# Two transformer layers over 16 sequences: the rotary of the second sequence on GpSimd, the squares of the first group's slots on ScalarE, the second group routed later

## The chip, the cores and the metric

The kernel runs on one core of one Trainium2 chip. The metric is the device time of one execution in microseconds (us). Three runs of the kernel before took 1694.8, 1696.43 and 1696.84 us; the median is 1696.43.

## The reference

`x` has 16 sequences of 512 tokens of width 128, in float32. Two layers follow each other. Each makes `x = x + attention(norm(x)) + ffn(norm(x))`.

```python
# layer 0
q, k, v = heads of xn @ Wq.T, xn @ Wk.T, xn @ Wv.T      # 16 heads of width 8
rot(x) = concat(x1 * c - x2 * s, x1 * s + x2 * c)       # rotary, halves of 4; of q and k
q, k = elu(rot(q)) + 1, elu(rot(k)) + 1
y_t = q_t . sum_{s<=t}(k_s v_s) / max(q_t . sum_{s<=t} k_s, 1e-6)     # linear attention, causal
combine = the two largest of softmax(xn @ router_w.T), made to sum to 1, over 8 experts
ffn = sum_e combine[e] * (relu(xn @ w_fc[e].T)**2 @ w_proj[e].T) + the shared expert, likewise
# layer 1
attention: softmax over chunks of 64 queries, a gate from its sums; ffn: a channel mix with the token before
```

Only layer 0 is touched by the change: its rotary, its routing to experts, and the order of its work.

## The kernel before, in words

**Tiling.** A sequence is four tiles of 128 tokens. The 16 sequences are handled in five groups of 3, 4, 4, 3 and 2 (`GROUPS`, line 47). Layer 0 of a group runs beside layer 1 of the group before it. Four chains of work make up the program (lines 1567 to 1595):

- `dispatch(g)` (line 1038) normalizes each sequence of a group (`layernorm_T`: tile `xn`, transposed to `xnT`), makes its router logits (`rt_ps`, `lg`), then routes the group as a whole. `route` (line 671) and `places` (line 718) compute, in some 60 small VectorE operations of at most 128x128, the slot of each token in the buffer of its two experts (`pl_slot`) and the expert of each slot tile (`pl_expert`). Then `send` (line 1087) writes each tile of `xn` to its slots in DRAM (`rows`) by an indirect DMA from GpSimd: 24 of them for group 0, 32 for group 1.
- `slot_tiles(g)` (line 1122) fetches four tiles of slots at a time (`xg`), transposes them (`xgT`), loads the weights of each tile's expert (`wf`, `wp`, 256 KB each, four buffers of each), multiplies (`hg_ps`), takes ReLU and squares (`hg`, in `hidden`, line 1164), multiplies again (`yg_ps`) and writes `results`. Group 0 has 31 such tiles.
- `layer0(g)` (line 1541) runs, sequence by sequence, `linear_operands` (line 827), `linear_attention` (line 917) and `shared_expert` (line 1006). The first two sequences run interleaved (`together`, line 1490), the second with buffers that layer 1 doesn't need yet (`LENT`, line 808).
- `layer1(g)` (line 1553) gathers the expert results back, and runs layer 1.

**The rotary** (lines 846 to 875). TensorE makes q, k and v of two tiles in PSUM (`qkv`). VectorE multiplies q and k by the cosine and by the sine table (`by_cos`, `by_sin`, 128x512 each), joins halves of these into `qr` by a subtraction and an addition (128x256 each), takes the minimum with zero (`phi`). ScalarE takes the exponential; VectorE adds it to the maximum with zero. This is done twice for each sequence. TensorE then makes running sums (`state`) and transposes (`qkT_ps`); scores (`sc`), masked by VectorE (`am`, 128x1024, eight for a sequence); outputs (`o`); transposes (`ho_a`), a division by VectorE (`den`, `o0n`), a transpose (`oh_a`) and the product `y`, with the shared expert's `h`.

**What sets the order.** Every operation is recorded, then emitted by a planner (`Program.run`, line 330) with costs in ns of its own (lines 213 to 222). An operation's rank is the order in which the chains recorded it; the chains are interleaved by due times (lines 1575 to 1583), which are counted in the planner's estimates of each group's length. At each step the planner emits the ready operation of lowest rank on the engine that is free first. On the chip every engine then runs its list strictly in order. So a changed operation or due time can move everything near it. An indirect DMA also waits for TensorE's instruction that was emitted last before it, and two of them are at least 1900 ns of the planner's time apart (line 222). All loads and stores are issued in order by one queue, that of SyncE (SP).

**Buffers.** `xn` has four: the normalization of a fifth sequence waits for the sends of the first. `x_in` has two. In the profile nearly every operation has the line 259, that of the recorder, so groups are told apart by their tiles.

Of the kernel before, what the change touches and what calls it, by code (L numbers as in the profile page):

```python
# [29 lines left out]
F32 = mybir.dt.float32  # L30
I32 = mybir.dt.int32
U32 = mybir.dt.uint32
AF = mybir.ActivationFunctionType
ALU = mybir.AluOpType
AX = mybir.AxisListType

P = 128
B, T, D = 16, 512, 128
# [448 lines left out]
def two_layers(ctx: ExitStack, tc: tile.TileContext, x, small, const, w_fc, w_proj, out):  # L487
    nc = tc.nc
    program = Program(tc)
    V, S, G, M, SP = (  # L490
        program.engine(name, api) for name, api in (
            ("DVE", nc.vector), ("ACT", nc.scalar), ("POOL", nc.gpsimd), ("PE", nc.tensor),
            ("SP", nc.sync),
        )
    )

    def pool(name, bufs, ahead=0, **kw):
        return Pool(
            ctx.enter_context(tc.tile_pool(name=name, bufs=bufs, **kw)), bufs, ahead,
            kw.get("space") == bass.MemoryType.PSUM,  # L500
        )

    fixed = pool("fixed", 1)
    p2 = pool("p2", 2)
# [5 lines left out]
    def big(name):  # L510
        return ps_big.tile([P, 2, 512], F32, tag="big", name=name)
# [16 lines left out]
    def load_x(b, tag, bufs):  # L528
# [4 lines left out]
    passed = {  # L533
        (n, b): memory.tile([P, T], F32, tag=f"{n}{b}", name=f"{n}_{b}")
        for n in ("xnT", "x1") for b in range(B) if n == "x1" or b > 1
    }
# [84 lines left out]
    def by_head(vp):  # L621
        return vp[:, :, 0 : H * (PAIR + 2)].rearrange("p t (h e) -> p t h e", e=PAIR + 2)
# [170 lines left out]
    def tokens_to_heads(o, name, tag):  # L793
# [14 lines left out]
    LENT = {  # L808
        "vpad": 2, "qr": ("ka", 2), "T": ("qa", "qa", 2), "q0m": ("probs", 4), "am": ("ka", 2),
        "oTs": "oTs1", "o": "o1n", "oT": "oT_a1", "xs": ("rr", 2),  # L810
    }
# [15 lines left out]
    def linear_operands(xnT, b, home):  # L827

        vp, vs, states = vpads[home["vpad"]], home["vstrips"], home["states"]
        vh = by_head(vp)
        tag, bufs = home["qr"]
        qr = p2.tile([P, NT, 2 * D], F32, tag=tag, name=f"qr_{b}", bufs=bufs)
        for tp in range(NT // 2):
            pq = big(f"qkv_{b}_{tp}")
            for i in range(2):  # L840
                t = 2 * tp + i
                M.matmul(
                    pq[:, i, 0 : 3 * D], xnT[:, t * P : (t + 1) * P],
                    wqkv0.rearrange("p s d -> p (s d)"), start=True, stop=True,
                )
            ts_ = slice(2 * tp, 2 * tp + 2)
            by_cos = p2.tile([P, 2, 2 * D], F32, tag="by_cos", name=f"by_cos_{b}_{tp}", bufs=1)
            by_sin = p2.tile([P, 2, 2 * D], F32, tag="by_sin", name=f"by_sin_{b}_{tp}", bufs=1)
            qk = pq[:, :, 0 : 2 * D].rearrange("p t (n d) -> p t n d", d=4)
            for o, table in ((by_cos, cos), (by_sin, sin)):  # L850
                V.tensor_tensor(
                    o.rearrange("p t (n d) -> p t n d", d=4), qk,
                    table[:, ts_, :].unsqueeze(2).to_broadcast([P, 2, 2 * H * 2, 4]), ALU.mult,
                )
            v = pq[:, :, 2 * D : 3 * D]
            S.copy(vs[:, ts_, :, 0:PAIR], v.rearrange("p t (s e) -> p t s e", e=PAIR))
            for o in range(2):
                S.copy(
                    vh[:, ts_, o::2, o * DH : (o + 1) * DH],
                    v.rearrange("p t (s o d) -> p t s o d", o=2, d=DH)[:, :, :, o, :],  # L860
                )

            def halves(a):
                return a.rearrange("p t (h two d) -> p (t h) two d", two=2, d=4)

            c, s, r = halves(by_cos), halves(by_sin), halves(qr[:, ts_, :])
            V.tensor_tensor(r[:, :, 0, :], c[:, :, 0, :], s[:, :, 1, :], ALU.subtract)
            V.tensor_tensor(r[:, :, 1, :], s[:, :, 0, :], c[:, :, 1, :], ALU.add)

            x = qr[:, ts_, :]  # L870
            ex = p2.tile([P, 2, 2 * D], F32, tag="by_cos", name=f"phi_{b}_{tp}", bufs=1)
            V.tensor_scalar_min(ex, x, 0.0)
            S.activation(ex, ex, AF.Exp)
            V.scalar_tensor_tensor(x, x, 0.0, ex, ALU.max, ALU.add)
            yield
        yield


        pst = one(f"state_{b}")
        for t in range(NT - 1):  # L880
            M.matmul(
                pst[:, 0 : 8 * (PAIR + 2)], qr[:, t, D : 2 * D],
                vs[:, t, :, :].rearrange("p s e -> p (s e)"),
                start=(t == 0), stop=(t == NT - 2), skip_group_check=True,
            )
            V.tensor_tensor(
                states[t][:, :, 0 : PAIR + 2],
                pst[:, 0 : 8 * (PAIR + 2)].rearrange("p (s e) -> p s e", e=PAIR + 2), blocks,
                ALU.mult,
            )  # L890
        yield

        pts = big(f"qkT_ps_{b}")
        for s in range(2):
            for t in range(NT):
                M.transpose(
                    pts[:, s, t * P : (t + 1) * P], qr[:, t, s * D : (s + 1) * D], ident
                )
        q_tag, k_tag, bufs = home["T"]
        qT = p2.tile([P, T], F32, tag=q_tag, name=f"q0T_{b}", bufs=bufs)  # L900
        S.copy(qT, pts[:, 0, :])
        kT = p2.tile([P, T], F32, tag=k_tag, name=f"k0T_{b}", bufs=bufs)
        S.copy(kT, pts[:, 1, :])
        qms = []
        for u in range(2):
            tag, bufs = home["q0m"]
            qm = (p3 if tag == "probs" else p2).tile(
                [P, 2, T], F32, tag=tag, name=f"q0m_{b}_{u}", bufs=bufs
            )
            for o in range(2):  # L910
                r = 2 * u + o
                S.activation(qm[:, o, :], pts[:, 0, :], AF.Copy, scale=c_("pick")[:, r : r + 1])
            qms.append(qm)
        yield
        return qT, kT, qms
# [206 lines left out]
    def slot_tiles(g):  # L1122
# [3 lines left out]
        _, n_slots = tiles_of(g)  # L1126
# [37 lines left out]
        def hidden(xgT, ws, q, pair):  # L1164
            ph = big(f"hg_ps_{g}_{q}_{pair}")
            for ii, (wf, _) in enumerate(ws):
                i = 2 * pair + ii
                for f in range(NF):
                    M.matmul(
                        ph[:, ii, f * P : (f + 1) * P], wf[:, f * P : (f + 1) * P],  # L1170
                        xgT[:, i * P : (i + 1) * P], start=True, stop=True,
                    )
            h = p2.tile([P, 2, FF], F32, tag="hid", name=f"hg_{g}_{q}_{pair}", bufs=4)
            o = h[:, 0 : len(ws), :]
            S.activation(o, ph[:, 0 : len(ws), :], AF.Relu)

            (V if pair or g == 0 else G).tensor_tensor(o, o, o, ALU.mult)
            return h

        def project(h, ws, n):  # L1180
# [17 lines left out]
        for q in range(-(-n_slots // QUAD)):  # L1198
# [3 lines left out]
            for pair in range(-(-n_quad // 2)):  # L1202
                n = q * QUAD + 2 * pair
# [306 lines left out]
    def head(b):  # L1510

        if not 0 <= b < B:
            return None
        x1 = p2.tile([P, NT, D], F32, tag="x1", name=f"x1_{b}")
        SP.dma_start(x1.rearrange("p t d -> p (t d)"), passed["x1", b])
        yield from combine(x1, b)
        xp = p2.tile([P, T + 1], F32, tag="xp", name=f"xp_{b}", bufs=2)
        G.memset(xp[:, 0:1], 0.0)
        yield from layernorm_T(x1, xp[:, 1 : T + 1], f"1_{b}", "xn1", 1)
        yield  # L1520
        base = yield from channel_mix(x1, xp, b)
        yield
        vp = values(xp[:, 1 : T + 1], b)
        yield
        qm, ka = yield from operands(xp[:, 1 : T + 1], b, 0)
        return xp, base, vp, qm, ka
# [45 lines left out]
    length = [a + b for a, b in zip(*work)]  # L1572
    begin = [sum(length[:g]) for g in range(groups + 1)]
    chains = [[], [], [], []]
    for g, n in enumerate(GROUPS):
        early, late = (begin[g - 1], length[g - 1]) if g else (-length[0], length[0])
        steps = n * (1 + NT) + 3
        chains[0].append((early + 0.1 * late, 0.4 * late / steps, dispatch(g)))
        start = begin[g] - 0.2 * late if g else 0.25 * length[0]
        steps = 5 * -(-tiles_of(g)[1] // QUAD) + 1  # L1580
        chains[1].append((start, (begin[g] + 0.8 * length[g] - start) / steps, slot_tiles(g)))
        chains[2].append((begin[g], length[g] / (n * LAYER_STEPS[0]), layer0(g)))
        chains[3].append((begin[g + 1], length[g + 1] / (n * LAYER_STEPS[1]), layer1(g)))
    jobs = [[c[0][0], c] for c in chains]
    while jobs:
        job = min(jobs, key=lambda j: j[0])
        _, step, steps = job[1][0]
# [102 lines left out]
```

## Time and profile before

The profiled execution took 1693.02 us, of which the span of the trace is 1691.2 (the rest lies ahead of the first and behind the last instruction). The busy time of each engine, in us, in stretches of the span:

| stretch, us | TensorE | VectorE | ScalarE | GpSimd | TensorE clock | DMA, GB/s |
|---|---|---|---|---|---|---|
| 0 to 50 | 22.23 | 36.29 | 15.49 | 12.73 | 0.77 | 174 |
| 50 to 100 | 40.64 | 30.87 | 15.38 | 18.78 | 0.85 | 116 |
| 100 to 150 | 40.19 | 29.21 | 17.12 | 21.51 | 0.86 | 182 |
| 150 to 200 | 49.28 | 25.18 | 17.13 | 15.24 | 1.00 | 239 |
| 200 to 250 | 45.56 | 26.71 | 21.76 | 18.44 | 1.00 | 214 |
| 250 to 300 | 47.04 | 45.28 | 21.07 | 20.40 | 0.93 | 199 |
| 300 to 1550 | 1207.18 | 939.34 | 603.27 | 299.31 | 0.99 | 88 |
| 1550 to 1691.2 | 118.50 | 88.81 | 53.49 | 5.75 | 0.86 | 10 |

How to read what follows. A timeline line gives the start, the duration, the engine, the operation with its tiles (output, arrow, inputs), the shape and the count, and in brackets the idle time of the engine just before and what ended it. The clock is the share of its full rate at which TensorE was let run: at 0.5 a product takes twice as long. DMA share is the mean busy share of 16 DMA engines. The indirect DMAs appear as work of GpSimd (POOL), about 1 us each. Layer 1 starts near 250 us.

### The profile page before, as it was taken

To read this page: it belongs to the slowest core of one execution; us is meant where nothing else is said; L and a number is where in the kernel's file an instruction comes from. 1 tells how busy PE (TensorE), PEld (TensorE's weight loads), DVE (VectorE), ACT (ScalarE), POOL (GpSimd) and SP (SyncE) were. 2 spreads that over 40 slices of the span, in tenths; PEclk is the share of its full clock that TensorE was granted. 3 is DMA by queue.
4 is the path that set the end of the run, shared out by engine and by line. 5 is a ranking of instruction groups with operands and counts; after the bars stand their busy time and mean duration, and the time that the engine had idled before them with its cause. 6 is when DMAs were issued, how large, how long until landed. Compare 5 with 4: busy or idle time off the path is not lost.

```text
span 1691.2 us, 36456 instructions
## 1 busy us (share of the span) xinstructions
PE 1570.6 (93%) x14503; PEld 1035.6 (61%) x14503; DVE 1221.7 (72%) x2520; ACT 764.7 (45%) x1175; POOL 412.2 (24%) x389
## 2 busy tenths in 40 slices
PE   4869999999999999999999999999999999999996
PEld 2658876576766566666666656666665566555443
DVE  7845458878478975986668894968587867677673
ACT  2324434544443644444444654453544543534424
POOL 2426053054114321151013321140115010104000
PEclk8879999999999999999999999999999999999888
DMA  5357775343342442332223242313133223010000
GB/s 166 119 165 227 219 223 177 94 128 106 110 117 88 116 144 70 111 109 77 88 78 95 80 129 76 103 55 117 51 90 92 63 72 100 8 45 28 19 1 13
DMA packets 155129, 167.78 MB, mean 99 GB/s; under 512 B 13264, under 2 KB 100688, under 8 KB 154960
## 3 DMA queue, kind: packets, MB, share of 16 engines
q1 hardware_dynamic: 146768, 148.67, 29.6%
q0 software_dynamic: 8192, 16.79, 3.1%
q8 instruction: 114, 1.87, 0.4%
q14 instruction: 55, 0.45, 0.1%
HBM read 123.59 MB, written 41.81 MB: 98 GB/s over the span
## 4 chain that ended last, share of the span: by engine, by line
PE 55%; DVE 12%; ACT 3%; issue 1%; ACTq 0%; DVEq 0%
PE sc L259 11%; PE o L259 10%; PE st L259 8%; PE yg_ps L259 5%; DVE maxima L259 4%; PE hg_ps L259 4%; PE y L259 4%; PE qk L259 3%; PE h_ps L259 2%; ACT ex L259 1%; PE ho_a L259 1%; PE qkv L259 1%; PE oh_a L259 1%; PE cm_r L259 1%; PE mx L259 1%
## 5 line engine op out<-in xcount | busy, mean ns | idle before, releaser
L259 DVE TENSOR_REDUCE maxima<-sc 128x2 f32<-128x768 f32 (+2 forms) x448 | 385.4, 913 | 73.9 <-PE sc L259 70.9
L259 ACT ACTIVATE ex<-st 128x1024 f32<-128x1024 f32 x320 | 312.4, 1025 | 184.8 <-PE st L259 175.5
L259 PE MATMUL sc<-ka,qa 32*128 32x512 f32 (+2 forms) x1792 | 213.8, 516 | 7.2 <-DVE maxima L259 3.5
L259 PE MATMUL st<-qa,ka 32*128 32x384 f32 (+3 forms) x2048 | 208.8, 466 | 9.2 <-ACT ex L259 4.6
L259 DVE TENSOR_TENSOR am<-sc,const_sb 128x1024 f32<-128x1024 f32 x128 | 151.3, 1218 | 86.4 <-PE sc L259 82.7
L259 PEld LDWEIGHTS yg_ps<-wp,hg 128*128 128x128 f32 x1304 | 161.9, 194 | 52.6 <-issue 33.4
L259 PE MATMUL yg_ps<-wp,hg 128*128 128x128 f32 x1304 | 184.1, 285 | 8.2 <-DVE hg L259 1.9
L1091 POOL DMA_INDIRECT rows<-xn,pl_slot x128 | 135.9, 1061 | 205.2 <-PE y L259 38.4
L259 PE MATMUL hg_ps<-xgT,wf 128*128 128x128 f32 x1304 | 176.9, 282 | 7.3 <-DVE maxima L259 2.4
L1110 POOL DMA_INDIRECT back<-results,pl_slot x128 | 129.6, 1013 | 213.9 <-PE st L259 45.5
L259 PEld LDWEIGHTS hg_ps<-xgT,wf 128*128 128x128 f32 x1304 | 160.1, 195 | 30.9 <-issue 13.6
L259 PE MATMUL o<-ex,vpad 128*32 128x512 f32 (+3 forms) x2048 | 174.6, 443 | 1.0 <-ACT oT_a L259 0.6
L259 PEld LDWEIGHTS st<-qa,ka 32*128 32x128 f32 x2048 | 103.3, 185 | 78.7 <-issue 27.9
L259 ACT ACTIVATE hg<-hg_ps 128x1024 f32<-128x1024 f32 x84 | 84.0, 1000 | 123.4 <-PE hg_ps L259 108.7
L259 POOL TENSOR_TENSOR hg<-hg 128x1024 f32<-128x1024 f32 x34 | 65.1, 1916 | 304.5 <-ACT hg L259 304.1
L259 PEld LDWEIGHTS sc<-ka,qa 32*128 32x128 f32 x1792 | 90.2, 187 | 68.8 <-issue 19.2
L259 PEld LDWEIGHTS o<-ex,vpad 128*32 128x32 f32 x2048 | 52.3, 109 | 87.4 <-issue 65.5
L259 ACT COPY oTs<-o 128x256 f32<-128x256 f32 (+1 forms) x96 | 42.7, 444 | 119.8 <-PE o L259 114.6
L259 DVE TENSOR_TENSOR hg<-hg 128x1024 f32<-128x1024 f32 (+1 forms) x50 | 58.3, 1167 | 45.6 <-ACT hg L259 38.6
L259 PE MATMUL sc<-q0m,k0T 32*128 32x256 f32 x1024 | 80.4, 405 | 1.8 <-ACT ex L259 1.3
L259 ACT COPY yg<-yg_ps 128x256 f32<-128x256 f32 x84 | 31.0, 369 | 110.5 <-PE yg_ps L259 87.5
L259 PE MATMUL o<-am,vpad 128*32 128x128 f32 x2048 | 77.9, 279 | 1.9 <-DVE am L259 1.8
(189 smaller groups left out, 2230.1 us busy)
## 6 DMA issues: line engine op xcount, KB each, us to landing
wf<-in_w_fc SPq DMA_DIRECT2D x163, 256.0 KB
wp<-in_w_proj SPq DMA_DIRECT2D x163, 256.0 KB
results<-yg SPq DMA_DIRECT2D x79, 128.0 KB
xg<-rows SPq DMA_DIRECT2D x37, 256.0 KB
rows<-zeros SPq DMA_DIRECT2D x2, 2496.0 KB
x_in<-in_x SPq DMA_DIRECT2D x16, 256.0 KB
x<-x SPq DMA_DIRECT2D x16, 256.0 KB
out<-rr SPq DMA_DIRECT2D x16, 256.0 KB
```

The source lines that it names most:

```text
L259: return getattr(api, method)(*map(made, args), **{k: made(a) for k, a in kw.items()})
L1091: i = nc.gpsimd.indirect_dma_start(out=rows.made()[:, :], out_offset=bass.IndirectOffsetOnAxis(ap=slot.made(), axis=0), in_=row.made(), in ...
L1110: "POOL", lambda: nc.gpsimd.indirect_dma_start(out=o.made(), out_offset=None, in_=results.made()[:, :], in_offset=bass.IndirectOffsetOnAxi ...
```

## The change

- For the second sequence (`LENT`), ScalarE copies q and k out of PSUM into `raw_qk` (GpSimd doesn't read PSUM here), and the two table products, the two half products and the minimum are GpSimd operations. Their buffers are those of `xr` and `xk`, which layer 1 uses from its start on, and `xs`, that of the first sequence's shared expert. The exponential stays on ScalarE, the last sum on VectorE.
- The square of each slot tile's ReLU in group 0 is an activation on ScalarE, right behind its ReLU, in the place of a VectorE product.
- The due time of group 1's `dispatch` goes from 0.1 to 0.3 of group 0's length, that of group 0's slot tiles from 0.25 to 0.4.
- An assertion at build time says that `x1` has been written before `head` reads it; it emits nothing.

By these the planner emits another order up to the product `y` of the third sequence: the rotary of the first sequence ahead of the routing of group 0; both attentions, the first shared expert with its product and the third sequence's rotary ahead of the first slot tile; the routing of group 1 behind it. On SP's queue the store of `x1` of the first sequence and its load for layer 1 stand ahead of the first `xg`. Behind that `y` the two programs have the same instructions in the same order on every engine.

```diff
@@ -844,11 +844,18 @@
                     wqkv0.rearrange("p s d -> p (s d)"), start=True, stop=True,
                 )
             ts_ = slice(2 * tp, 2 * tp + 2)
-            by_cos = p2.tile([P, 2, 2 * D], F32, tag="by_cos", name=f"by_cos_{b}_{tp}", bufs=1)
-            by_sin = p2.tile([P, 2, 2 * D], F32, tag="by_sin", name=f"by_sin_{b}_{tp}", bufs=1)
-            qk = pq[:, :, 0 : 2 * D].rearrange("p t (n d) -> p t n d", d=4)
+            X, n_c, n_s = V, "by_cos", "by_sin"
+            qk = pq[:, :, 0 : 2 * D]
+            if home is LENT:
+                X, n_c, n_s = G, "xr", "xk"
+                raw_qk = p2.tile([P, 2, 2 * D], F32, tag="xs", name=f"raw_qk_{b}_{tp}", bufs=1)
+                S.copy(raw_qk, qk)
+                qk = raw_qk
+            by_cos = p2.tile([P, 2, 2 * D], F32, tag=n_c, name=f"by_cos_{b}_{tp}", bufs=1)
+            by_sin = p2.tile([P, 2, 2 * D], F32, tag=n_s, name=f"by_sin_{b}_{tp}", bufs=1)
+            qk = qk.rearrange("p t (n d) -> p t n d", d=4)
             for o, table in ((by_cos, cos), (by_sin, sin)):
-                V.tensor_tensor(
+                X.tensor_tensor(
                     o.rearrange("p t (n d) -> p t n d", d=4), qk,
                     table[:, ts_, :].unsqueeze(2).to_broadcast([P, 2, 2 * H * 2, 4]), ALU.mult,
                 )
@@ -864,12 +871,12 @@
                 return a.rearrange("p t (h two d) -> p (t h) two d", two=2, d=4)
 
             c, s, r = halves(by_cos), halves(by_sin), halves(qr[:, ts_, :])
-            V.tensor_tensor(r[:, :, 0, :], c[:, :, 0, :], s[:, :, 1, :], ALU.subtract)
-            V.tensor_tensor(r[:, :, 1, :], s[:, :, 0, :], c[:, :, 1, :], ALU.add)
+            X.tensor_tensor(r[:, :, 0, :], c[:, :, 0, :], s[:, :, 1, :], ALU.subtract)
+            X.tensor_tensor(r[:, :, 1, :], s[:, :, 0, :], c[:, :, 1, :], ALU.add)
 
             x = qr[:, ts_, :]
-            ex = p2.tile([P, 2, 2 * D], F32, tag="by_cos", name=f"phi_{b}_{tp}", bufs=1)
-            V.tensor_scalar_min(ex, x, 0.0)
+            ex = p2.tile([P, 2, 2 * D], F32, tag=n_c, name=f"phi_{b}_{tp}", bufs=1)
+            X.tensor_scalar_min(ex, x, 0.0)
             S.activation(ex, ex, AF.Exp)
             V.scalar_tensor_tensor(x, x, 0.0, ex, ALU.max, ALU.add)
             yield
@@ -1174,7 +1181,10 @@
             o = h[:, 0 : len(ws), :]
             S.activation(o, ph[:, 0 : len(ws), :], AF.Relu)
 
-            (V if pair or g == 0 else G).tensor_tensor(o, o, o, ALU.mult)
+            if g == 0:
+                S.activation(o, o, AF.Square)
+            else:
+                (V if pair else G).tensor_tensor(o, o, o, ALU.mult)
             return h
 
         def project(h, ws, n):
@@ -1512,6 +1522,7 @@
         if not 0 <= b < B:
             return None
         x1 = p2.tile([P, NT, D], F32, tag="x1", name=f"x1_{b}")
+        assert passed["x1", b].base.writers
         SP.dma_start(x1.rearrange("p t d -> p (t d)"), passed["x1", b])
         yield from combine(x1, b)
         xp = p2.tile([P, T + 1], F32, tag="xp", name=f"xp_{b}", bufs=2)
@@ -1575,8 +1586,8 @@
     for g, n in enumerate(GROUPS):
         early, late = (begin[g - 1], length[g - 1]) if g else (-length[0], length[0])
         steps = n * (1 + NT) + 3
-        chains[0].append((early + 0.1 * late, 0.4 * late / steps, dispatch(g)))
-        start = begin[g] - 0.2 * late if g else 0.25 * length[0]
+        chains[0].append((early + (0.3 if g == 1 else 0.1) * late, 0.4 * late / steps, dispatch(g)))
+        start = begin[g] - 0.2 * late if g else 0.4 * length[0]
         steps = 5 * -(-tiles_of(g)[1] // QUAD) + 1
         chains[1].append((start, (begin[g] + 0.8 * length[g] - start) / steps, slot_tiles(g)))
         chains[2].append((begin[g], length[g] / (n * LAYER_STEPS[0]), layer0(g)))
```

## The prediction, made before the changed kernel was run

> **What bounds the kernel now.** First the page's busy rows and slices, then a table by stage, then the timeline of the first stage.
>
> ```profile
> PE 1570.6 (93%) x14503; PEld 1035.6 (61%) x14503; DVE 1221.7 (72%) x2520; ACT 764.7 (45%) x1175; POOL 412.2 (24%) x389
> ...
> PE   4869999999999999999999999999999999999996
> ...
> PEclk8879999999999999999999999999999999999888
> ```
>
> TensorE is the engine that is full, from the fourth slice (127 us) on. What it loses is in the first three slices, and there its clock is low too. The table by stage puts numbers on this (us; busy time and, in brackets, instructions of each engine; then granted clock, DMA share, GB/s):
>
> ```profile
> 17.80:42.50 24.70, 8.44 (x28) 4.94 (x26) 21.18 (x82) 8.08 (x21) 2.12 (x2) 0.69 0.25 77
> 54.60:95.60 41.00, 32.16 (x455) 24.02 (x455) 26.54 (x58) 8.91 (x21) 16.33 (x17) 0.92 0.24 76
> 95.60:125.00 29.40, 19.75 (x111) 18.18 (x112) 16.99 (x68) 7.72 (x12) 5.80 (x5) 0.71 0.63 183
> ...
> 240.06:1691.20 1451.14, 1381.35 (x12822) 878.30 (x12820) 1080.44 (x2157) 681.93 (x1019) 331.31 (x300) 0.98 0.29 85
> 95.60:240.06 144.46, 130.75 (x1137) 113.80 (x1138) 75.59 (x142) 54.29 (x95) 49.33 (x42) 0.94 0.71 217
> ```
>
> Up to 42.5 us VectorE is 86% busy and TensorE waits. From 54.6 to 95.6 TensorE is 78% and VectorE 65% busy, each waiting for the other in turn. From 95.6 to 125 TensorE is idle for a third at a clock of 0.71. After 240 us it is 95% busy. The timeline names the waits:
>
> ```profile
> 40.08 1.18 POOL L1091 DMA_INDIRECT rows<-xn,pl_slot  x1 [31.29 <-DVE pl_ef L259]
> ...
> 44.15 1.28 ACT L259 ACT_TABLE_LOAD   x1 [13.72 <-DVE phi L259]
> ...
> 91.52 1.12 DVE L259 TENSOR_SCALAR xn<-x_in,ln_mv,ln_rstd 128x128 f32<-128x128 f32 x4 [6.71 <-DMA rows<-xn,pl_slot]
> ...
> 95.61 1.73 PE L259 MATMUL xgT_ps<-const_sb,xg 128*128 128x128 f32 x7
> ...
> 117.04 1.09 PE L259 MATMUL oh_a<-const_sb,o0n 128*128 128x128 f32 x4 [6.54 <-DVE o0n L259]
> ```
>
> VectorE makes the rotary of both sequences and the routing of group 0 in one queue: slots at 40 us, the second half of sequence 0's rotary only at 46. The 24 row sends last from 40.08 to 90.12, and the first slot tile follows at 95.61. Then VectorE routes group 1 ahead of the first squares and of the attention's divisions, and TensorE stands.
>
> **The point to which I count.** Both programs can be set side by side instruction by instruction. From the first product of sequence 2's shared expert on (before: `y` at 240.06) all engines have the same instructions in the same order: 3179 of TensorE's 3550 rows, 1850 of VectorE's, the last 253 of GpSimd's. So the change can gain or lose only ahead of that point, and what it shifts there reaches the end nearly whole, since the rest is TensorE-bound. Noise of the rest: a few us.
>
> **The change part by part.**
>
> *Rotary on GpSimd.* VectorE loses, for each of two halves, by_cos and by_sin (0.69 each), two half products (0.42) and the minimum (0.42): 2.64, 5.3 in all. ScalarE gets two copies of 128x512 out of PSUM (0.59 each by the xnT row) ahead of the exponentials; it is a third busy there. GpSimd gets ten operations. Its nearest rows are rr plus x, 128x512 from two tensors: 1.27 us; one-input 128x512: 0.62. So a half costs 2x1.27 + 2x0.72 (half size, estimate from 1.27 and 0.62) + 0.62 = 4.6, both 9.2. The trace has no GpSimd operation with such a broadcast table; bounds: 7.5 (by the 1.04 of a square) and 18 (double); below 7.5 nothing is near. I take 9.2. [...]
>
> *Does GpSimd work beside VectorE for nothing?* No:
>
> ```profile
> 235.32 1.90 POOL L259 TENSOR_TENSOR hg<-hg 128x1024 f32<-128x1024 f32 x1
> 235.57 1.81 DVE L259 SCALAR_TENSOR_TENSOR x<-back,rt_m,x 128x128 f32<-128x128 f32 x1 [1.11 <-DMA back<-results,pl_slot]
> ...
> 252.36 0.34 DVE L259 SCALAR_TENSOR_TENSOR x<-back,rt_m,x 128x128 f32<-128x128 f32 x1
> ```
>
> The same VectorE form takes 0.34 alone and 1.81 when it meets GpSimd: it stands until GpSimd ends. [...] Routing is full of 128x96 products from two SBUF tensors. [...] VectorE gets in between GpSimd's operations and has some waits of its own, so I take 5.5.
>
> *Order in VectorE's queue.* Ahead of the slots now stand, in addition, the rest of sequence 0's rotary (0.84+0.42+0.68), sequence 1's last product (0.68) and six state products (0.3 each): +4.4; gone from there is half of sequence 1's rotary: -2.6. Slots at 39.9 + 1.8 + 5.5 = 47. The last product waits for GpSimd and ScalarE's exponential, and the whole of the slot computation stands behind it: GpSimd should be done near 34, VectorE asks near 40, 6 us of slack. With the lock gone: slots at 41.7; with it in full: 51.
>
> *First slot tile.* The sends are tied to TensorE's progress; at before's pace (50.0 us for 24, then 5.5 to the transposes) it starts at 47 + 50 + 5.5 = 102.5. Bounds 97 and 110. That is 7 later than before. But both attentions, the closing transposes, sequence 0's shared expert and product, and sequence 2's rotary products now stand ahead of it: h 3.6, ho and oh 2.2, qkv 2.6, y 4.6, state and qkT 1.9, some 15 us that before does after 95.6. TensorE has room for them: 32.2+15 = 47 us of work between 49 and 102. SP's queue carries the write and read-back of x1 of sequence 0 ahead of the first xg; its product ends before the last send, so nothing is added.
>
> *From there to the common point.* Before: 144.5 us, busy 130.75, of which 6.5 is slow clock ahead of 125 us (19.75 busy where the same forms at the full clock make 13.2); so 124 of work and 20 lost. After: 124 - 15 = 109. The 20 lost came from group 1's routing standing ahead of squares and divisions; squares (16 of 1.22 on VectorE) go to ScalarE at about 1.0 each (its ReLU of 128x1024: 1.02), the divisions are done before, and routing has the attention of sequence 2 beside it. ScalarE is 38% busy there and would be at 60%; two more table loads (1.28 each) are hidden likewise. I leave 9.5 lost: 4 at the pace of 125 to 240 us (4 idle in 115), the rest a cold start and the first wait for routing and weights.
>
> *Group 1 later.* Its 32 sends start later, but its first rows are asked for only after them in TensorE's order, near group 0's last tiles; SP's queue would stop there, with weights behind it. They took 64 us before, and some 80 lie between. Nothing added.
>
> Sum: 102.5 + 109 + 9.5 = 221 against 240: 19 us less. The profiled execution took 1693.0 (span 1691.2), the median is 1696.4; so 1674 as a profile, **1677.5** as a median.
>
> **Rivals.**
>
> *Weights set the pace (1689).* The stage moved 217 GB/s x 144.5 = 31.4 MB. In 119 us this is 264 GB/s; the best 20 us of the stage before had 241 (220 to 240 us). If 241 is what these requests can do, it takes 130 us: common point at 232.5, gain 7.5. Against it: stretches of 5 us reach 346, and from 140 to 180 TensorE was full at a DMA share of 0.75.
>
> *The lock costs its whole length and more (1687).* Slots at 56: ten more, gain 9 or so.
>
> *Sends follow a faster TensorE (1668).* No lock, first tile at 97, 6 lost: gain 28.
>
> *Slower: routing waits for GpSimd (1703).* Sequence 1's last product stands in VectorE's queue ahead of the slots. Every us that GpSimd's ten operations end after 40 delays slots, sends and first tile by one. [...] At 31 us late the kernel is 6 slower.
>
> **How the numbers follow.** Likeliest 0.50 (1670 to 1686), weights 0.14, lock 0.12, faster sends 0.12, slower 0.12. Range 1666 to 1694. A change under 0.2% (3.4 us) can't be told from none: faster 0.80, same 0.08, slower 0.12.
>
> **What would show it.** GpSimd rows by_cos of about 1.3 us and VectorE routing products stretched beside them; slots at 45 to 50; first slot tile at 99 to 106; no idle of 6 us before oh; the common point at 215 to 228; the rest of the span unchanged within 3 us. It is wrong if the first tile comes after 115, if TensorE waits on weights for over 10 us, or if the tail moves though its order does not.

## The result, and the profile after

The changed kernel took 1690.0, 1688.96, 1684.67 and 1685.18 us: median 1687.07, where the kernel before has 1696.51 over four runs. The ratio is 0.995, with a 95% interval of 0.9931 to 0.9969: 9.4 us faster (5 to 12 by the interval), where 19 were forecast. The profiled execution of after took 1690.0 us, a span of 1688.2, so the two profiled ones differ by only 3.0; why that is less than 9.4 comes below.

Of the page of after, the busy times and slices:

```profile
PE 1572.5 (93%) x14503; PEld 1033.7 (61%) x14503; DVE 1201.6 (71%) x2494; ACT 783.9 (46%) x1195; POOL 415.8 (25%) x399
...
PE   5889789999999999999999999999999999999986
...
PEclk8989999999999999999999999999999999999887
```

The third slice of TensorE (84 to 127 us) went from 6 to 8, but the fifth (169 to 211 us), full before, is at 7. The table by stage of after (us; busy time and instructions of PE, PEld, DVE, ACT, POOL; then granted clock, DMA share, GB/s):

```profile
50.00:102.27 52.27, 44.67 (x513) 33.14 (x507) 39.59 (x95) 16.37 (x36) 21.28 (x22) 0.89 0.37 118
...
102.27:125.00 22.73, 21.92 (x181) 17.82 (x182) 12.46 (x29) 11.53 (x17) 0.00 (x0) 0.88 0.98 287
...
180.00:212.00 32.00, 23.42 (x171) 22.56 (x172) 0.00 (x0) 13.02 (x20) 5.57 (x6) 0.89 0.73 219
...
102.27:234.87 132.60, 117.59 (x1058) 103.48 (x1058) 45.68 (x102) 62.45 (x95) 43.83 (x42) 0.95 0.78 234
234.87:1688.00 1453.13, 1380.82 (x12822) 876.77 (x12820) 1079.09 (x2157) 681.96 (x1019) 329.93 (x300) 0.98 0.29 85
```

From 50 us to the first slot tile TensorE is busy for 44.7 us where before had some 36. Behind it the stage takes 132.6 us to the common point, the start of the third sequence's `y`; the forecast had 118.5. That point comes at 234.87, 5.2 us earlier than before's 240.06, where 19 were forecast. From 180 to 212 us VectorE does nothing and TensorE is idle for a quarter. The timeline of the start:

```profile
20.57 1.04 POOL L259 TENSOR_TENSOR by_cos<-raw_qk,const_sb 128x512 f32<-128x512 f32 x1 [11.98 <-ACT raw_qk L259]
...
21.63 2.55 DVE L259 TENSOR_SCALAR xn<-x_in,ln_mv,ln_rstd 128x128 f32<-128x128 f32 x3
...
24.18 1.68 POOL L259 TENSOR_SCALAR phi<-qr 128x512 f32<-128x512 f32 x1
...
44.87 0.17 DVE L259 CAST pl_slot<-pl_slotf 128x12 uint32<-128x12 f32 x1
...
45.91 1.20 POOL L1098 DMA_INDIRECT rows<-xn,pl_slot  x1 [11.76 <-DVE pl_ef L259]
...
102.27 1.09 PE L259 MATMUL xgT_ps<-const_sb,xg 128*128 128x128 f32 x4 [0.90 <-DMA xg<-rows]
```

GpSimd begins at 20.57, 0.08 us after its copy has ended. Three `xn` of 128x128 take 2.55 us beside its products; in the run below with the rotary undone, where GpSimd is idle, four take 1.11. And here is where the stage loses, first TensorE, then ScalarE (columns: start, duration, idle before and its releaser):

```profile
186.58 0.94 PE L259 MATMUL yg_ps<-wp,hg 128*128 128x128 f32 x6 [1.87 <-ACT hg L259]
...
189.36 1.06 PE L259 MATMUL hg_ps<-xgT,wf 128*128 128x128 f32 x8
192.62 1.40 PE L259 MATMUL yg_ps<-wp,hg 128*128 128x128 f32 x6 [2.20 <-ACT hg L259]
```

```profile
190.45 1.02 ACT L259 ACTIVATE hg<-hg_ps 128x1024 f32<-128x1024 f32 x1 [0.52 <-issue]
191.51 1.06 ACT L259 ACTIVATE hg<-hg 128x1024 f32<-128x1024 f32 x1
```

TensorE ends the products of a pair at 190.4, ScalarE takes ReLU and square in a row until 192.6, and TensorE has nothing but this pair's projection to do. Call such a pair bare. TensorE stands like this five times in the stage, for 9.7 of its 15.0 us of idle time. At four of the five (8.0 us) ScalarE had itself been idle for 0.5 us when it began the ReLU, as here:

```profile
204.16 1.02 ACT L259 ACTIVATE hg<-hg_ps 128x1024 f32<-128x1024 f32 x1 [0.52 <-PE hg_ps L259]
206.32 1.45 PE L259 MATMUL yg_ps<-wp,hg 128*128 128x128 f32 x6 [2.20 <-ACT hg L259]
```

So there it is the length of the two operations in series that TensorE waits for, and no other work in ScalarE's queue.

### The profile page after: what moved, and what is told of

Read it like the earlier page. It is cut to its first block, busy times and chain, and to the rows that moved or that the text cites. A ratio compares the mean times of both kernels' runs of the same rounds, so it can differ in the third digit from the quotient of the medians.

```text
span 1688.2 us, 36448 instructions
## 1 busy us (share of the span) xinstructions
PE 1572.5 (93%) x14503; PEld 1033.7 (61%) x14503; DVE 1201.6 (71%) x2494; ACT 783.9 (46%) x1195; POOL 415.8 (25%) x399
## 4 chain that ended last, share of the span: by engine, by line
PE 55%; DVE 12%; ACT 3%; issue 1%; ACTq 0%; DVEq 0%
PE sc L259 11%; PE o L259 10%; PE st L259 8%; PE yg_ps L259 5%; DVE maxima L259 4%; PE hg_ps L259 4%; PE y L259 4%; PE qk L259 3%; PE h_ps L259 2%; ACT ex L259 1%; PE qkv L259 1%; PE ho_a L259 1%; PE oh_a L259 1%; PE cm_r L259 1%; PE mx L259 1%
## 5 line engine op out<-in xcount | busy, mean ns | idle before, releaser
L1098 POOL DMA_INDIRECT rows<-xn,pl_slot x128 | 130.5, 1020 | 198.4 <-PE y L259 38.8
L259 ACT COPY oTs<-o 128x256 f32<-128x256 f32 (+1 forms) x96 | 42.6, 444 | 123.3 <-PE o L259 121.5
L259 PE MATMUL y<-wpj_s,h 128*128 128x128 f32 x512 | 75.7, 285 | 0.4 <-DVE h L259 0.4
```

The source lines that it names most:

```text
L259: return getattr(api, method)(*map(made, args), **{k: made(a) for k, a in kw.items()})
L1098: i = nc.gpsimd.indirect_dma_start(out=rows.made()[:, :], out_offset=bass.IndirectOffsetOnAxis(ap=slot.made(), axis=0), in_=row.made(), in ...
```

## The experiments

**How they are compared.** They ran in four sets, each on one chip beside the kernel before: its median was 1696.1, 1696.4, 1689.1 and 1696.7 us. So ratios to before are compared across sets, and times within a set. "At 400 us" is how much earlier than in before's profile the same DMA of the queue SP starts there: at that point all kernels have the stage behind them, and the same order of instructions from there on. For the changed kernel it is 8.5 us, and from 405 to 1592 us it stays between 8.1 and 8.5. Such instants also hold what differs between chips: before's profile is a single execution, and before's median is 7 us lower on the chip of the third set.

**Theory:** the time that the forecast missed is lost at bare pairs, where the pair's latency (ReLU and square, 2.1 us) has nothing beside it. **Rivals:** the weights set the pace; ScalarE's queue does, since it has the squares; the rotary's lock does (in before VectorE took 1.81 us beside GpSimd for what takes 0.34 alone).

### First set: the pair, the weights, the squares, the tiles' due time

*Short squares.* In the changed kernel's own order on every engine:

```diff
-                S.activation(o, o, AF.Square)
+                # planned at the cost of before, made on [:, :, 0:16]
+                nc.scalar.activation(small, small, AF.Square)
```

> The changed kernel in its own order on every engine, but ScalarE squares only 16 of the 512 columns of each tile of group 0 (the rest stays the ReLU), so a pair of tiles is ready about 0.85 us sooner. Theory (the lost time is TensorE standing at pairs of slot tiles that have nothing between them and their projection): the waits of yg on ScalarE's hg fall from 9.7 us to about 5, the common point comes 4 to 6 us earlier than 234.9, time near 1682. Rival (weights set the pace): what is won at one wait is lost at the next weights, common point within 1.5 us, time near 1687.

Measured: 1684.23 us, ratio 0.993 (0.9913 to 0.9947). Common point at 228.55, 6.3 earlier, of which 1.3 lie ahead of the first tile (101.0) and 5.0 in the stage; at 400 us 13.9 earlier than before, 5.4 more than the change. The waits of yg on hg fell from 9.7 to 3.0. The theory holds, in size too, by the trace; the ratio alone isn't told apart from the change.

*Half the weights*, same order, same products:

```diff
-    wf.made(), w_fc[:, bass.ds(e, 1), :]
+    wf.made()[:, 0 : a * P], w_fc[:, bass.ds(e, 1), 0 : a * P]      # a = 2 of 4 for group 0; wp likewise
```

> The changed kernel in its own order on every engine, but for group 0 only half of each expert's weights is loaded (the products use that half twice, as many products as before). Theory (bare pairs): TensorE's waits stay as they are, common point at 233 to 236, time 1685 to 1689. Rival (weights set the pace): the stage's bytes fall by over a third and with them the lost time, common point 8 or more us earlier, time near 1678.

Measured: 1691.1 us, ratio 0.9966 (0.9953 to 0.9979), so nothing is won. The stage moved 181 GB/s instead of 234, a quarter less (not over a third, as the rival had it), and took 131.9 us instead of 132.6. TensorE's waits in it, of after and then of this run (us in total, times, longest):

```profile
PE yg_ps L259 <- ACT hg L259: 9.7, 5, 2.2
PE yg_ps L259 <- ACT yg L259: 1.9, 2, 1.0
```

```profile
PE yg_ps L259 <- ACT hg L259: 9.7, 5, 2.2
PE yg_ps L259 <- ACT yg L259: 1.9, 2, 1.0
```

They are the same waits. The weights don't set the pace of the changed kernel. (It stands 4 us above the changed kernel's first median for what comes behind the stage: 7.0 us ahead of before at 400 us, 1.0 at the end; see the clock below.)

*Squares on VectorE again:*

```diff
-            if g == 0:
-                S.activation(o, o, AF.Square)
-            else:
-                (V if pair else G).tensor_tensor(o, o, o, ALU.mult)
+            (V if pair or g == 0 else G).tensor_tensor(o, o, o, ALU.mult)
```

> The changed kernel with one part undone: the squares of group 0 on VectorE again (1.22 us each where ScalarE took 1.06). Theory (bare pairs, whoever squares): the bare pairs stay in the order, each wait is 0.2 longer, and squares meet the routing of group 1 in one queue: 1 to 4 us slower than the changed kernel, 1688 to 1691. Rival (it is ScalarE's queue, with ReLU, square and copies in a row, that makes TensorE stand): 3 to 5 us faster, 1682 to 1684.

Measured: 1687.73 us, ratio 0.9954 (0.9938 to 0.997): as the changed kernel. Neither expectation is met well: TensorE waits 3.6 us on hg and 3.3 on xgT, the stage is shorter (125.5 us, 11.7 earlier at 400 us), and in the median none of that is seen. The planner writes another order for it, so this isn't the squares' price alone.

*Slot tiles due at 0.25 again:*

```diff
-        start = begin[g] - 0.2 * late if g else 0.4 * length[0]
+        start = begin[g] - 0.2 * late if g else 0.25 * length[0]
```

> The changed kernel with one part undone: the slot tiles of group 0 due at 0.25 of the group's length again, not 0.4. In TensorE's order the first tile then stands 29 rows earlier and more of the attention is left between later pairs. Theory (bare pairs): the time lost behind the first tile falls from 20 to some 14 us, while the first tile, held by the row sends, comes at 97 to 103 all the same: common point near 229, time near 1681. Rival (weights set the pace): common point within 2 us of 235, time 1686 to 1688. If instead the tiles ahead of the attention make TensorE stand for the rows, as before, it is slower, 1690 to 1693.

Measured: 1696.99 us, ratio 1.0007 (0.9994 to 1.0019): the whole gain is gone. The theory's numbers failed; of the last sentence the direction came, and more of it. The stages of this run:

```profile
50.00:94.64 44.64, 33.42 (x431) 25.16 (x427) 27.21 (x69) 10.58 (x25) 20.11 (x21) 0.84 0.42 132
94.64:234.38 139.74, 129.64 (x1137) 110.66 (x1138) 57.83 (x130) 71.67 (x112) 45.96 (x45) 0.98 0.75 226
```

Bare pairs cost it little (3.0 us on hg), and the first tile comes at 94.6. But TensorE is busy for 33 us ahead of it and 130 behind it, where the change has 45 and 118. So the due time does two things at once: it takes 12 us of work out of the stage, and cover out of its pairs. Up to the third sequence's `y` the two cancel: it starts at 234.4, with the change at 234.9. This run falls behind only after that point (at 400 us it is 2.2 us earlier than before, the change 8.5), where its order still differs up to some 340 us and its clock is lower (0.95 from 234 to 338 us; the change has 0.98 from 235 to 332). How much of the 6.3 us each of these takes is open.

### Second set: the other parts, and the planner's pace

*Rotary on VectorE again:*

```diff
-            if home is LENT:
+            if home is None:      # never, here
                 X, n_c, n_s = G, "xr", "xk"
```

> The changed kernel with one part undone: the second sequence's rotary on VectorE, as before; squares on ScalarE and the later due times stay. Theory (the gain comes from the later due time of the slot tiles, which puts 13 us of TensorE's work ahead of them; the rotary's new place gives little, since VectorE stands for GpSimd): slots back at 40 us, first slot tile at 96 to 101, time within 2.5 us of the changed kernel, 1685 to 1690. Rival (the rotary on GpSimd carries the gain): 1694 or more.

Measured: 1683.6 us, ratio 0.9921 (0.99 to 0.9942). Slots at 40.77, first tile at 95.88; 15.5 us earlier at 400 us, nearly twice the change. The theory is right that the rotary doesn't carry the gain, but with the squares on ScalarE its new place isn't worth little, it costs. The lock isn't what the stage loses: without it TensorE is still idle for 14.1 us of a stage of 128.6, and waits 5.9 on hg.

*Routing of group 1 due at 0.1 again:*

```diff
-        chains[0].append((early + (0.3 if g == 1 else 0.1) * late, ...
+        chains[0].append((early + 0.1 * late, ...
```

> The changed kernel with one part undone: the routing of group 1 due at 0.1 again, not 0.3. Theory: it stands in VectorE's queue ahead of the attention's divisions again, TensorE stands some 6 us in front of one product ahead of the slot tiles or behind the first of them, and 3 to 6 us of the gain go: 1690 to 1693. Rival (VectorE has room for it wherever it stands): 1685 to 1688.

Measured: 1695.83 us, ratio 0.9998 (0.9984 to 1.0012). More than expected: all of the gain is gone. The waits of its stage show the old one again beside the new ones:

```profile
PE yg_ps L259 <- ACT hg L259: 8.2, 6, 2.2
PE oh_a L259 <- DVE o0n L259: 8.0, 1, 8.0
```

*Rotary on GpSimd alone*: the kernel before, with of the change only its first two hunks, in short

```diff
+            if home is LENT:
+                X, n_c, n_s = G, "xr", "xk"
```

> The kernel before with one part of the change done: the rotary of the second sequence on GpSimd; squares on VectorE and the due times as before. Theory: slots come 0 to 4 us later than before's 39.0 (half a rotary less ahead of them, the stretched routing more), the 6.5 us in front of oh stay, and nothing of the gain is there: 1694 to 1699. Rival (the rotary carries the gain): 1690 or less.

Measured: 1697.8 us, ratio 1.0004 (0.9992 to 1.0016). Slots at 42.6, 3.6 later; the 6.5 us in front of oh are there.

*The planner's pace*: the planner counts weights at half their bytes, the loads are as before.

```diff
-            program.add("SP", emit, [expert.base], [wf.base, wp.base], 300.0, 4.0 * P * 2 * FF)
+            program.add(..., 300.0, (2.0 if g == 0 else 4.0) * P * 2 * FF)
```

> The changed kernel, but the planner that writes the order counts the weights of group 0 at half their bytes; the loads themselves are unchanged. In its order the next pair's first products then mostly stand between a pair and its projection: by counting rows, 2.3 us of cover are missing 11.5 us in all where the changed kernel misses 19.8. Theory (bare pairs are the lost time, and the planner's pace for weights makes them): 3 to 5 us faster than the changed kernel, 1682 to 1684. Rival (the weights do come at the planner's pace): the waits turn into waits for wf, time 1686 to 1688.

Measured: 1687.82 us, ratio 0.9939 (0.9921 to 0.9958), which is not told apart from the change. Common point at 230.9, 11.1 us earlier at 400 us (2.6 better than the change), with no wait on ScalarE's hg among the larger ones and a new one:

```profile
PE hg_ps L259 <- DMA wf<-in_w_fc: 4.4, 5, 2.4
PE yg_ps L259 <- ACT yg L259: 3.3, 3, 1.6
```

So the rival isn't dead: the weights are the next limit as soon as the pairs are covered.

### Third set: the due times alone, and the change beside them

*Due times alone*, on the kernel before:

```diff
+        chains[0].append((early + (0.3 if g == 1 else 0.1) * late, ...
+        start = begin[g] - 0.2 * late if g else 0.4 * length[0]
```

> The kernel before with one part of the change done: only the two later due times (routing of group 1 at 0.3, slot tiles of group 0 at 0.4); rotary and squares on VectorE. Theory (the due times carry the gain, the rotary's new place costs some 4 us at the slots, the squares' place little): slots near 41, first slot tile at 95 to 98, 1682 to 1687, within 2.5 us of the kernel that has only its rotary undone (1683.6). Rival (squares on VectorE meet the late routing and the parts are needed together): 1690 or more.

Measured: 1677.36 us, ratio 0.9941 (0.9923 to 0.9959); slots at 40.95, first tile at 94.67. The absolute number was expected from a chip on which before takes 7 us more, so the ratio counts; it lies where the theory's 1682 to 1687 put it (0.9915 to 0.9945).

*Squares alone*, on the kernel before:

```diff
+            if g == 0:
+                S.activation(o, o, AF.Square)
```

> The kernel before with one part of the change done: only the squares of group 0 on ScalarE. Theory: the 6.5 us in front of oh stay, since group 1's routing still stands ahead of the divisions; 1693 to 1698. Rival (VectorE was late because of the squares): 1690 or less.

Measured: 1691.49 us, ratio 1.0015 (1.0001 to 1.0028), nothing won; the wait in front of oh is 6.0.

*Split pairs*, with the rotary on VectorE:

```diff
+    # tile 0: ReLU and Square on ScalarE; tile 1: on VectorE, in a buffer of its own
+    V.tensor_scalar_max(o, ph[:, 1, :], 0.0)
+    V.tensor_tensor(o, o, o, ALU.mult)
```

> The changed kernel with its rotary on VectorE again, and with each pair of group 0 made in two tiles side by side: ReLU and square of the first on ScalarE, of the second on VectorE, so that a pair is ready some 0.8 us sooner. Theory (bare pairs): the waits of yg on hg fall from 5.9 us to 3 or less, 2 to 4 us faster than the same kernel without it (1683.6): 1679.5 to 1682. Rival (planner's pace and weights take it up again): 1683 to 1685.

Measured: 1680.43 us, ratio 0.995 (0.9932 to 0.9968). The theory's number failed: the waits on hg rose to 9.8 us (5.7 on VectorE's half, one of 4.8), since that half stands in one queue with group 1's routing. The ratio isn't told apart from that of the same kernel without the split (0.9921). A shorter latency doesn't help if it is put behind other work.

*The changed kernel again:*

> The changed kernel again, unaltered, beside the other three. Every theory: 1685 to 1689. If the last 5 us of difference between single executions come from the granted clock behind the common point, the profile again shows a stretch of low clock behind 1580 us or near 930 to 1010, and the instants from 400 to 900 us agree with the first profile within 1 us.

Measured: 1682.3 us, ratio 0.9966 (0.9953 to 0.9979). The stage is reproduced: 132.87 us where the first profile had 132.60, waits on hg of 9.3 where it had 9.7. The first slot tile is not: it comes at 98.4 for 102.3, and the common point at 231.25. It is 9.3 us earlier than before's profile at 400 us, within 1 us of the first; at 800 us it is 12.4, which the theory didn't have (the chip is another one), and near 1000 us the clock falls, as expected at one of the two places. On this chip the due times alone are 4.9 us faster.

With both due times late, the ratios of the four combinations are:

| | squares on VectorE | squares on ScalarE |
|---|---|---|
| rotary on VectorE | 0.9941 | 0.9921 |
| rotary on GpSimd | 0.9954 | 0.995 and, again, 0.9966 |

With the squares on VectorE the intervals don't tell the rotary's new place from nothing. With them on ScalarE it costs: the second measuring of the change lies clear of 0.9921, the interval of the first overlaps that of 0.9921. The squares' place can't be told from nothing in either row.

### Fourth set: what is left

*Pair ready at once*, same order: ReLU on 128 of 512 columns, square on 16, the projection reading those 128 four times.

```diff
-    S.activation(o, ph[:, 0 : len(ws), :], AF.Relu)
+    # planned at full cost, made on [:, :, 0:P]; the square on [:, :, 0:16]
```

> The changed kernel in its own order on every engine, but for group 0 ScalarE takes the ReLU of only 128 of the 512 columns of each tile and squares 16 of them (the projections read those 128 columns four times, as many products as before): a pair is ready 0.6 us after its products, not 2.1. If the pair's latency is the whole of the time that TensorE stands in the stage, its waits on hg go to nothing, idle falls from 15 us to under 7, and the time is 2 to 4 us below the run with short squares alone (ratio to before near 0.991). If another limit is next (weights, copies of the rows), waits of that kind take its place and the time is that of the short squares (ratio 0.993).

Measured: 1683.06 us, ratio 0.9919 (0.9905 to 0.9932). Its stage, and the waits in it:

```profile
102.03:224.59 122.56, 114.85 (x1057) 100.66 (x1058) 45.61 (x102) 40.92 (x96) 43.26 (x42) 0.98 0.83 252
```

```profile
PE xgT_ps L259 <- DMA xg<-rows: 2.8, 2, 1.8
PE yg_ps L259 <- POOL hg L259: 1.7, 2, 1.4
PE yg_ps L259 <- ACT hg L1190: 1.5, 2, 0.7
```

Same order, same products, first tile within 0.3 us of the change, and the stage is 10.0 us shorter: 7.3 of idle time (15.0 to 7.7) and 2.7 of slow clock. In the time only some 5 us of that (0.9919 against 0.995) arrive.

*Slot tiles due at 0.33*, rotary and squares on VectorE:

```diff
-        start = begin[g] - 0.2 * late if g else 0.4 * length[0]
+        start = begin[g] - 0.2 * late if g else 0.33 * length[0]
```

> The kernel before with the routing of group 1 due at 0.3 and the slot tiles of group 0 due at 0.33 of the length, not 0.4 (rotary and squares on VectorE). By counting rows, the cover missing between pairs and projections is 12.3 us where the one with 0.4 misses 17.2, but less work stands ahead of the first tile. Theory (work that is put ahead of the tiles is the cover that later pairs miss): the two cancel in good part, ratio 0.993 to 0.997, within 0.002 of the 0.994 of the due times alone. Rival (bare pairs alone count): better, 0.991 or below.

Measured: 1685.69 us, ratio 0.9929 (0.9916 to 0.9943): within 0.002 of 0.9941, and not told apart from it. So far as expected of cover against work moved; the rival's 0.991 lies just outside the interval.

*Due times and the planner's weights at three quarters*, rotary and squares on VectorE:

```diff
-            300.0, 4.0 * P * 2 * FF)
+            300.0, (3.0 if g == 0 else 4.0) * P * 2 * FF)
```

> The kernel before with the two later due times alone, and the planner counting the weights of group 0 at three quarters of their bytes: cover missing falls from 17.2 us to 12.2 by counting rows, with the same work ahead of the first tile. Theory: waits on hg fall by 3 to 5 us, ratio 0.990 to 0.993. Rival (waits on weights take their place, as they did in part with the pace at half): 0.993 to 0.996.

Measured: 1682.57 us, ratio 0.9914 (0.9899 to 0.9929). The furthest ahead of all at 400 us (18.9 earlier), with the third sequence's `y` at 218.4 (in its order 24 products that before makes ahead of `y` stand behind it), and the best ratio, faster than both kernels; from the due times alone (0.9941) the intervals don't tell it quite apart. Waits on hg fell from 7.9 to 1.4 us, and waits on wf rose from 0.6 to 5.1.

## Why the prediction was right on the start and wrong on the stage

**Right: the start.** Slots were put at 47 and came at 44.87, the first slot tile at 102.5 and came at 102.27 (the sends took as long as before). That the second is so close is in part luck: the five profiles with this order have it between 98.4 and 102.3. GpSimd's ten operations took 10.6 us for the 9.2 forecast, and VectorE did stand beside them: the three `xn` above for some 1.7 us (2.55 against 0.83, three quarters of the 1.11), and four of the routing's 128x96 products took 2.57 us where the same four take 1.04 in before, with GpSimd idle. So what the forecast read from 0.34 and 1.81 us is borne out for these rows. The 5.5 us that its sum has for it was my estimate, and no run shows it: the rows named are 3.2 us longer together. What the sum did not do is price this part alone. The undone rotary says it: slots at 40.8 instead of 44.9, first tile 6.4 us sooner, ratio 0.9921 against 0.995; on one chip, due times alone against all of it (the squares differ too), 4.9 us. Over all profiles the slots lie at 42.6 to 44.9 us with this rotary on GpSimd and at 39.0 to 41.0 with it on VectorE. How much of the 4.1 is lock and how much order wasn't separated.

**Right: the wait in front of oh**, 6.5 us, is gone, by the later routing: undone, it is back with 8.0 us and takes the gain with it.

**Nearly right: the work moved ahead.** I took 15 us off 124. Measured are 117.6 busy, of which 5.2 is slow clock (21.9 at 0.88 and 23.4 at 0.89), so 112.4, not 109.

**Wrong: "I leave 9.5 lost: 4 at the pace of 125 to 240 us (4 idle in 115), the rest a cold start and the first wait for routing and weights."** This is the term that failed. Lost were 20.2: 15.0 idle and 5.2 slow clock. The sum is 112.4 + 20.2 = 132.6 for the 109 + 9.5 = 118.5 of the forecast, 14.1 us; 10.0 of these go away when a pair is ready at once (7.7 idle and 2.3 slow clock are then lost, about the 9.5 that I left), and 3.4 are the work above. I took the pace of before over into a stage from which the change takes what made that pace: the attentions and products that stood between a pair's first products and its projection were the "15 us of work" that I moved ahead of the tiles. The same microseconds were counted twice, as work gone and as cover still there. The order of the changed kernel, counted by rows, showed pairs with next to nothing between them. And ScalarE, put at "60%" as if a share of busy time told of latency, was busy 62.45 of 132.6, 47%, while it held TensorE up.

**The rivals.** *Weights set the pace* forecast a common point at 232.5 and a gain of 7.5, close to 234.9 and 9.4, by a cause that isn't there: half the bytes change nothing, and 252 GB/s were moved when pairs were ready at once, above the 241 that I took for its ceiling. It becomes true at another point, when the pairs are covered. *The lock costs its whole length* was right in its sign and put the slots at 56; they came at 45. *Routing waits for GpSimd* didn't come: GpSimd ended at 34.2, near the forecast 34, where 31 us late would be 65.

**The rest of the span** moved by 2 us between the two profiles, though its order didn't, which I had allowed ("within 3 us"). But the 2 us are the sum of two larger shifts, and neither belongs to the change. First, the lead grows from 5.2 us at the common point to 8.5 at 400 us. Of this, 2.8 us arise at once, over the same 117 products, of before and then of after:

```profile
240.06:260.00 19.94, 17.50 (x117) 15.41 (x116) 16.76 (x52) 8.29 (x14) 11.60 (x11) 0.83 0.62 190
```

```profile
234.87:252.00 17.13, 14.24 (x117) 12.96 (x116) 15.03 (x52) 8.32 (x14) 11.72 (x11) 1.00 0.71 217
```

TensorE's clock is 0.83 in one and 1.00 in the other. In the other four profiles with this order the lead changes between the two instants by -0.8 to 2.3 us, so most of the 3.3 belongs to these two executions and not to the order. Second, the lead falls from 8.2 us at 1592 us to 2.9 at 1656. These are windows of the same instructions, of before and then of after:

```profile
1642.19:1652.06 9.87, 9.32 (x89) 4.21 (x82) 8.18 (x17) 3.17 (x5) 0.00 (x0) 1.00 0.00 0
1652.06:1662.05 9.99, 9.65 (x100) 5.42 (x103) 4.89 (x7) 5.88 (x7) 0.00 (x0) 1.00 0.10 29
```

```profile
1635.64:1647.93 12.29, 11.75 (x89) 5.02 (x82) 9.13 (x17) 3.07 (x5) 0.00 (x0) 0.78 0.01 2
1647.93:1659.11 11.18, 10.85 (x100) 5.81 (x103) 3.72 (x5) 5.88 (x7) 0.00 (x0) 0.89 0.08 23
```

The 189 products take 19.9 us at a clock of 1.00 and 23.5 at 0.78 and 0.89. So the profiled pair shows 3.0 us where the medians show 9.4 (before's profiled 1693.0 lies 3.5 below its median, after's 1690.0 lies 2.9 above its own). What the sum explains is the 5.2 us at the common point; the medians' 9.4 has an interval from 5 to 12, and the second set has 0.9966, 6 to 7 us. That the first median came to half of the forecast, and not to a quarter, isn't explained by its sum.

## What to carry to other kernels

Work that is moved out from between two dependent steps is also the cover of the second: before "work gone" is taken off a stage, list what then stands between each producer and consumer there and compare it with the latency in series (here 2.1 us, of which TensorE stood 1.6 to 2.2 at each of the five bare pairs, so that hardly anything was covered). Of a change in several parts, price each part alone: here the two due times alone made the whole gain, either of them undone took all of it away (for the slot tiles' due time, why is open), and the rotary on the second engine cost 5 us or more with the squares on ScalarE, and with the squares on VectorE nothing that the noise would show. And a limit that is cleared by an experiment is cleared for this order only: the weights were no limit until the pairs were covered.

## What the runs showed of the hardware that was not expected

**The same instructions were granted a clock of 1.00 once and of 0.62 once.** Near 1000 us both profiles of the changed kernel run the same instructions, with the same waits of at most 0.9 us. The first profile, then the second:

```profile
1000.00:1005.00 5.00, 4.42 (x42) 1.85 (x41) 4.80 (x8) 1.46 (x3) 0.00 (x0) 1.00 0.00 0
1005.00:1010.00 5.00, 4.03 (x40) 2.37 (x41) 2.10 (x7) 4.88 (x5) 0.00 (x0) 1.00 0.00 0
```

```profile
996.00:1001.00 5.00, 4.37 (x42) 1.95 (x42) 4.76 (x9) 1.46 (x3) 0.00 (x0) 1.00 0.00 0
1001.00:1006.00 5.00, 4.08 (x26) 2.39 (x29) 1.20 (x5) 4.49 (x5) 0.00 (x0) 0.62 0.00 0
```

One goes on at full clock, the other falls to 0.62 with TensorE 82% busy, and 2.8 us of its lead are gone by 1100 us. Such places lie, by the lowest of the 5-us windows of nine profiles, near 500 us (0.70 to 0.79, in four of them), 580 (0.50 to 0.79, in all), 930 (0.71 to 0.78, in three), 1000 (0.50 to 0.60, in five) and behind 1550 us (0.50, in all). So which of them fall differs between executions, on one chip too: from 880 to 1100 us half the weights, with windows at 0.71 and 0.50, lost 4.4 us of its lead, and short squares, on the same chip, none. Such falls give back up to 9 us of a front's gain: the run with due times and pace is 18.9 us ahead at 400 us and 9.6 ahead at the end (by its 5-us windows it loses some 8 us more to slow clock there than before does). What decides at which of them the clock falls stays open.

**GpSimd's products with a broadcast table** took 1.04, 1.04, 1.12 and 1.43 us at 128x512, where the forecast took 1.27 from the trace of before; and its one-input minimum 1.49 and 1.68 us beside VectorE, where 0.62 was the row for it.
